# Attention and a mixture of experts on one core: three chunks of the last sequence sorted by expert, and VectorE adding the last weights

## The chip, the core and the metric

The kernel runs on one NeuronCore of a Trainium2 chip. A core has a matrix engine (TensorE, PE in the profile; its weight loads are PEld) and three engines for elementwise work: VectorE (DVE), ScalarE (ACT) and GpSimd (POOL). SyncE (SP) computes nothing here: it issues DMAs, and GpSimd issues the indirect ones. Each engine executes its own instructions in order and waits on semaphores for the others. SBUF is the on-chip memory with 128 partitions; PSUM, which the matmuls write, has eight banks of 128 x 512 fp32.

The metric is the time of one execution on the device in microseconds (us), taken as the median over runs.

## What is computed

All data is fp32: B = 4 sequences of S = 1024 tokens with D = 512 features, 16 heads of 32, and E = 8 experts of rank R = 64.

```python
x = _layernorm(x + _L0_attn_ref(x, wq, wk, wv, wo))   # softmax(q k^T) v, without a scale, then wo
logits = x_flat @ Wr.T + br                           # (4096, 8)
probs = softmax(logits)
expert_idx, expert_weight = argmax(probs), max(probs)
h = einsum('nd,erd->ner', x_flat, A)                  # A: (8, 64, 512)
y = einsum('ner,eor->neo', h, B) / 64                 # B: (8, 512, 64)
x = _layernorm(x + y[n, expert_idx[n]] * expert_weight)
```

A token needs one expert only. The reference computes all eight and picks one; a kernel may sort the tokens by expert, so that a tile of 128 tokens needs the weights of one expert, or multiply by all eight (E x R = 512 columns, as wide as D) and mask what isn't wanted.

## The kernel before

**Names.** A *unit* u is one sequence b and one group g of four heads, u = 4b + g, 16 in all; LAST = 12 is the first unit of the last sequence. A *query chunk* c or n is QC = 256 tokens; a sequence has four (NQ), and eight key tiles of 128 (NK). N = 272.

**The main loop** (L1000 to L1018) goes over steps i. A step does, in this order on every engine's queue: `early[i]` (loads on SP), `ahead[i]`, `weigh(i - 16)`, `scores(i)`, then, on every fourth step (a *busy* step), `settle` of four steps ago and `combine`, then `small[i]`, and last `fill[i]`. `keep_order` fixes the order in which the program issues the instructions as the order of each engine, so a waiting instruction holds up all that stands behind it on its engine.

- `scores(s)` computes 128 x 512 scores for each of the four heads of a unit (L290) and their row maxima on VectorE (L292). Only the maxima are kept. There are 256 such steps, 0 to 255; after step 255 there are none.
- `weigh(s)` computes the scores again, the other way round and with the maxima already subtracted: four matmuls put the negated maxima into four banks (L321), sixteen add key tile by queries (L330), and four exps on ScalarE (L340) write two key tiles of weights, `probs` (4 buffers). GpSimd adds the weights up into `dens`: one add of 128 x 1024 for the first pair of key tiles (L343), two for each later pair (L351). `weigh(s)` stands at step s + 16, so it runs in steps 16 to 271.
- `added(u, c)` says how many of the eight key tiles GpSimd adds: all, but six in the last chunk of the last sequence. `settle` sums `dens`, and with it the tiles that were not added, over the partitions by matmuls with ones (L385), and VectorE takes the reciprocal (L388) and scales the attention output `both` to `aT` (L390).
- `combine` multiplies weights and values on PE (L366) and copies the result to `both` (L374).
- `fill[i]` holds *pieces*: projections and the expert work. A planner (L916 to L955) puts each piece at a step between its `first` and its `last`, so that the steps get a similar number of PE cycles; `SHORTEST` is the least level that it fills a step to. A piece's `then` list puts further calls into the `small` (or `ahead`) list of a step so many steps later.

In sequences 0 to 2 the chunks of one unit follow each other; in the last sequence all four units do chunk 0, then all do chunk 1, and so on (L206, L208). Chunk n of the last sequence is therefore complete about every 16 steps: chunk 0 near step 224, chunk 3 at step 272.

**Sequences 0 to 2** (class `After`). `load` takes the tokens x from DRAM into tiles of tag "h" (8 buffers of 128 x 514: 512 features, the gate, and the token's place in the output). `project` adds the attention output times wo; `norm`, `choose` and `gate` layernorm two tiles, choose the expert and write the gate. When all eight tiles are done, `count` works out for every token its row in the order of experts: matmuls with a triangle of ones (L507 to L516), then some fifteen small VectorE operations, which give the row numbers `slot` and for every sorted tile its expert, `whose` (L551). `scatter` writes a tile by an indirect DMA on GpSimd's queue to the DRAM tensor `sorted_x[b]`, of NX = 16 tiles of 128 rows: a tile holds tokens of one expert, and rows that no token takes hold a place that lies out of bounds, because 1 MB writes from `nothing` were issued before (L839 to L842).

The sorted tiles are then done in pairs. For pair k: `load_tokens` reads two tiles back into buffers of tag "h" (SP, and it waits for all scatters), `load_up` and `load_down` read the expert's number into an SP register (`value_load`) and load that expert's weights, `turn_tokens` transposes on PE (L601) with copies on ScalarE, `up` (L608) and `down` (L617) multiply, and VectorE adds (L620). A step piece (`step(x)`) does `up` of pair x - 1, `down` of pair x - 2 and `turn_tokens` of pair x. The pair that had its `down` gets `weigh_y` (statistics on VectorE, `rs` on GpSimd) in the `ahead` list one step later, `norm_y` (ScalarE) two steps later and `store`, two indirect DMAs on GpSimd's queue, three steps later.

**The last sequence** (class `Last`). Each of the four chunks is done with all experts. Two chunks at a time lie in the place of `wv` (`places["h"]`), which is no longer needed. After `project`, `norm` and the choice, `turn` transposes the chunk, four `up` pieces multiply with all of `wu` (512 columns, L715), `turn_one` and `mask` spread the choice over the columns (L723) and multiply, four `down` pieces multiply with `wd` (L730), and `finish` layernorms and writes the tokens to `out` in order, by plain DMAs on SP.

Of the kernel before, what the change touches and what calls it, by code (L numbers as in the profile page):

```python
# [41 lines left out]
def attention_then_experts(  # L42
# [62 lines left out]
    wq_sb, load_wq = weight("wq", wq)  # L105
# [60 lines left out]
    sorted_x = [dram.tile([NX * P, W], F32, tag=f"sorted{b}", name=f"sorted{b}") for b in range(B - 1)]  # L166
# [146 lines left out]
    def weigh(s):  # L313
# [25 lines left out]
        for j, ps in enumerate(tiles):  # L339
            act.activation(pr[:, :, j, :], ps.rearrange("p (k q) -> p k q", q=QC), AF.Exp)  # L340
        if kp == 0:
            dens[u, c] = work.tile([P, GH * QC], F32, tag="dens", name="dens")
            pool.tensor_add(  # L343
# [4 lines left out]
        else:  # L348
            for k in range(2):
                if 2 * kp + k < added(u, c):  # L350
                    pool.tensor_add(dens[u, c], dens[u, c], pr[:, k].rearrange("p j q -> p (j q)"))  # L351

    def added(u, c):

        return NK if u < LAST or c < NQ - 1 else NK - 2
# [104 lines left out]
    class After:  # L460


        def __init__(self, b):
            self.b = b
            self.h, self.mv, self.rs, self.raw, self.ex = {}, {}, {}, {}, {}
# [4 lines left out]
        def load(self, n):  # L470
            for t in (TQ * n, TQ * n + 1):
                h = self.h[t] = work.tile([P, W], F32, tag="h", name="h", bufs=NT)
# [21 lines left out]
        def choose(self, n):  # L494
            if n == 0:
                self.one = work.tile([P, NT + 1, E], BF16, tag="one", name="one", bufs=1)
                pool.memset(self.one[:, NT], 0.0)
            self.ex[n] = choose(self.raw[n], self.one[:, ts(n, TQ), :])
# [4 lines left out]
        def count(self):  # L503

            whole = bank()
            ps = whole[:, : (NT + 1) * E].rearrange("p (t e) -> p t e", e=E)
            pe.matmul(ps, before, self.one, start=True, stop=False)  # L507
            for t in range(NT):
# [3 lines left out]
                    self.one[:, t, :].unsqueeze(1).to_broadcast((P, NT - t, E)),  # L512
                    start=False,
                    stop=(t == NT - 1),
                )

            at = [(NT + 1) * E]

            def room(n):
                at[0] += n  # L520
                return whole[:, at[0] - n : at[0]]

            tiles, place, slot, whose = room(E), room(2 * E), room(NT), room(NX)
            every = (P, NT, E)
# [3 lines left out]
                ps[:, NT, :].unsqueeze(2).to_broadcast((P, E, NT)),  # L528
# [6 lines left out]
            base = work.tile([P, E], F32, tag="base", name="base")  # L535
            dve.tensor_copy(base, place[:, :E])
            dve.tensor_add(ps[:, :NT], ps[:, :NT], base.unsqueeze(1).to_broadcast(every))
            dve.tensor_mul(wide[:, :NT], ps[:, :NT], self.one[:, :NT])
            dve.tensor_reduce(slot, wide[:, :NT], axis=AX.X, op=ALU.add)
            self.slot = work.tile([P, NT], U32, tag="slot_i", name="slot_i")  # L540
            dve.tensor_copy(self.slot, slot)

            dve.tensor_tensor(
                wide[:, :, : E - 1],
                place[:, E : 2 * E - 1].unsqueeze(1).to_broadcast((P, NX, E - 1)),
# [22 lines left out]
        def load_tokens(self, k):  # L568
            assert len(self.scatters) == NT
# [75 lines left out]
        def step(self, x):  # L645

            if 0 <= x - 1 < NT:
                self.up(x - 1)
            if 0 <= x - 2 < NT:
                self.down(x - 2)  # L650
            if x < NT:
                self.turn_tokens(x)

    places = {}

    class Last:


        def __init__(self, n):
            self.n = n  # L660
            self.h = [places["h"][:, (TQ * n + i) % C, :] for i in range(TQ)]
# [124 lines left out]
    for i, (u, c, kp) in enumerate(weights):  # L786
# [3 lines left out]
        elif kp == KP - 1:  # L790
            later(i + NS + 1, 3 * 4 * QC, settle, i)
# [23 lines left out]
    for n in range(1, NQ):  # L815
        for pair in ((0, 1), (2, 3)):
# [5 lines left out]
            for g in pair:  # L822
                Piece(lambda g=g, x_in=x_in: project_q(LAST + g, x_in), HALF, first, last, load=x_in)
# [11 lines left out]
    rest = [After(b) for b in range(B - 1)]  # L835
    for b, r in enumerate(rest):
        end = start_of(C * b + C)
        for i in range(4):
            part = sorted_x[b].rearrange("(i j p) w -> i p j w", p=P, i=4)[i]  # L839
            early[start_of(b * C + i) + 6].append(  # L840
# [3 lines left out]
        for t in range(NT):  # L844
            n, i = divmod(t, TQ)
            for half in range(2):
                then = []
                if i == TQ - 1 and half == 1:
                    then = [(2, 0, r.norm, n), (3, 0, r.choose, n), (4, 0, r.gate, n)]
# [206 lines left out]
```

## Time and profile before

| what | value |
|---|---|
| time, median of 3 runs | 1501.81 us (1500.35 to 1504.54) |
| the profiled execution | 1507.33 us |
| its span, first to last instruction | 1505.6 us |
| granted TensorE clock, mean over the span | 0.993 of full speed |
| GpSimd's adds of weights, L351 | 376 of 2358 ns: 886.6 us |
| GpSimd's adds of weights, L343 | 64 of 2355 ns: 150.7 us |
| VectorE's maxima, L292 | 1024 of 683 ns: 636.1 us |
| ScalarE's exps, L340 | 1024 of 603 ns: 528.1 us |

The page of a profile gives each engine's busy time and its share of the span, then the groups of instructions by line. A record reads, for instance, "L601 MATMUL bank<-ident,x": line 601, output `bank`, inputs `ident` and `x`; then partitions x elements of each, the type, and how many records (x8). In a timeline a row begins with its start and its length in us, and may end with the idle time before it and what ended that. A table by stretch gives the busy time of every engine between two points of the span.

### The profile page before, as it was taken

Reading aid. Unit: us, or ns where it says so; the run is one execution under the profiler, and the core shown is the slowest. Engines: PE = TensorE matmul, PEld = TensorE weight load, DVE = VectorE, ACT = ScalarE, POOL = GpSimd, SP = SyncE. Lnnn points to the kernel's source line nnn. Section 1 sums busy time; section 2 is a strip of 40 time slices with the busy share of each in tenths; the row PEclk is TensorE's granted clock in tenths of the full one; section 3 lists DMA queues with packets and bytes.
Section 4 is the critical chain, followed back from the end, with each engine's and each line's share of the span. In section 5 each row is a group of like instructions: output and inputs, shape, how many; then the busy total and the mean of one; then the engine's idle time right before and its main releaser. Section 6 shows DMA issues by size and latency. Waiting matters only on the chain. (4 is left out here: it accounts for less than half of the span.)

```text
span 1505.6 us, 36958 instructions
## 1 busy us (share of the span) xinstructions
PE 1463.2 (97%) x15091; PEld 953.4 (63%) x15091; DVE 960.0 (64%) x1797; ACT 741.7 (49%) x1519; POOL 1210.5 (80%) x935
## 2 busy tenths in 40 slices
PE   8999999999999999999999999999999999999986
PEld 6666666666665666666666666666666566666655
DVE  2546666666666567676676557677678667786523
ACT  1125555554444565555444455555554555556631
POOL 2019999998877889899887798999998899899850
PEclk9999999999999999999999999999999999999998
DMA  7422212122101522442111252441310221122100
GB/s 238 140 84 72 70 45 72 44 85 85 57 16 57 191 84 82 132 134 75 40 43 39 89 176 68 133 126 50 126 58 30 92 93 51 42 86 73 37 2 28
DMA packets 93050, 122.09 MB, mean 81 GB/s; under 512 B 7607, under 2 KB 68039, under 8 KB 92880
## 3 DMA queue, kind: packets, MB, share of 16 engines
q1 hardware_dynamic: 84672, 103.93, 21.6%
q0 software_dynamic: 6096, 13.69, 2.5%
q8 instruction: 119, 1.95, 0.5%
q10 hardware_dynamic: 2112, 2.10, 0.4%
q14 instruction: 51, 0.42, 0.1%
HBM read 92.34 MB, written 33.63 MB: 84 GB/s over the span
## 5 line engine op out<-in xcount | busy, mean ns | idle before, releaser
L351 POOL TENSOR_TENSOR dens<-dens,probs 128x1024 f32<-128x1024 f32 x376 | 886.6, 2358 | 100.9 <-ACT probs L340 79.4
L292 DVE TENSOR_REDUCE top<-bank 128x1 f32<-128x512 f32 x1024 | 636.1, 683 | 425.3 <-PE bank L290 424.8
L340 ACT ACTIVATE probs<-bank 128x512 f32<-128x512 f32 x1024 | 528.1, 603 | 272.7 <-PE bank L330 261.0
L290 PE MATMUL bank<-k,q 32*128 32x512 f32 x2048 | 286.9, 594 | 3.3 <-DVE whose_i L551 3.3
L330 PE MATMUL bank<-q,k 32*128 32x256 f32 x4096 | 266.6, 374 | 0.0
L366 PE MATMUL bank<-probs,v 128*32 128x256 f32 x4096 | 236.6, 383 | 0.0
L330 PEld LDWEIGHTS bank<-q,k 32*128 32x128 f32 x4096 | 201.5, 184 | 17.4 <-issue 1.9
L366 PEld LDWEIGHTS bank<-probs,v 128*32 128x32 f32 x4096 | 130.9, 111 | 95.1 <-ACT probs L340 14.6
L343 POOL TENSOR_TENSOR dens<-probs 128x1024 f32<-128x1024 f32 x64 | 150.7, 2355 | 18.0 <-ACT probs L340 17.8
L257 PE MATMUL bank<-xT,wq 128*128 128x256 f32 x512 | 128.5, 395 | 7.6 <-DMA xT<-in_xt 7.0
L388 DVE RECIPROCAL bank<-bank 128x256 f32<-128x256 f32 x64 | 112.6, 1759 | 33.2 <-PE bank L385 33.0
L290 PEld LDWEIGHTS bank<-k,q 32*128 32x128 f32 x2048 | 111.6, 184 | 27.8 <-DVE whose_i L551 5.8
L257 PEld LDWEIGHTS bank<-xT,wq 128*128 128x128 f32 x512 | 93.7, 192 | 54.8 <-ACT probs L340 33.1
L446 PE MATMUL bank<-wo,aT 128*128 128x264 f32 (+1 forms) x512 | 122.1, 390 | 5.6 <-ACT probs L340 4.6
L267 PE MATMUL bank<-xT,wk 128*128 128x256 f32 x512 | 123.5, 386 | 3.2 <-ACT probs L340 3.1
L276 PE MATMUL bank<-wv,xT 128*128 128x256 f32 (+1 forms) x512 | 124.5, 391 | 1.2 <-ACT probs L340 0.4
L446 PEld LDWEIGHTS bank<-wo,aT 128*128 128x128 f32 x512 | 94.6, 190 | 41.6 <-ACT probs L340 26.0
L267 PEld LDWEIGHTS bank<-xT,wk 128*128 128x128 f32 x512 | 95.2, 191 | 36.8 <-ACT probs L340 25.0
L374 ACT COPY both<-bank 128x256 f32<-128x256 f32 x64 | 23.8, 372 | 191.4 <-PE bank L366 175.7
L276 PEld LDWEIGHTS bank<-wv,xT 128*128 128x128 f32 x512 | 93.8, 190 | 36.1 <-ACT probs L340 19.2
L321 PE MATMUL bank<-mT,ones_b 3*128 3x512 bf16 x1024 | 106.0, 385 | 1.3 <-ACT probs L340 0.3
L321 PEld LDWEIGHTS <-ones_b 3*128 3x128 bf16 x1024 | 26.9, 91 | 91.0 <-issue 90.8
(123 smaller groups left out, 969.2 us busy)
## 6 DMA issues: line engine op xcount, KB each, us to landing
xT<-in_xt SPq DMA_DIRECT2D x98, 512.0 KB, 3.5
sorted<-nothing SPq DMA_DIRECT2D x12, 1028.0 KB, 6.6
x<-sorted SPq DMA_DIRECT2D x48, 257.0 KB, 3.6
h<-in_x SPq DMA_DIRECT2D x32, 256.0 KB, 3.7
wa<-in_wa SPq DMA_DIRECT2D x48, 128.0 KB, 2.2
wb<-in_wb SPq DMA_DIRECT2D x48, 128.0 KB, 3.4
out<-h SPq DMA_DIRECT2D x8, 256.0 KB, 2.0
wo<-in_wo POOLq DMA_DIRECT2D x1, 1024.0 KB, 6.3
```

The source lines that it names most:

```text
L257: pe.matmul(ps, wq_sb[:, c, ts(units[u][1], P)], x.x[:, c, :], start=(c == 0), stop=(c == C - 1))
L267: pe.matmul(ps, wk_sb[:, c, ts(units[u][1], P)], x.x[:, c, :], start=(c == 0), stop=(c == C - 1))
L276: pe.matmul(ps, x.x[:, c, ts(t, P)], wv_sb[:, c, columns(h)], start=(c == 0), stop=(c == C - 1))
L290: pe.matmul(ps, q[r, ts(t % TQ, P)], kT[u][r, ts(n, 512)], start=True, stop=True)
L292: dve.tensor_reduce(top[i][:, here // 2, j, n : n + 1], ps, axis=AX.X, op=ALU.max, negate=True)
L321: pe.matmul(ps.rearrange("p (k q) -> p k q", q=QC), ones_b[r, :], m[r, :].unsqueeze(1).to_broadcast((NP, 2, QC)), start=True, stop=False,)
L330: pe.matmul(ps[:, ts(k, QC)], kT[u][r, ts(2 * kp + k, P)], qT[u, c][r, :], start=False, stop=(k == 1),)
L340: act.activation(pr[:, :, j, :], ps.rearrange("p (k q) -> p k q", q=QC), AF.Exp)
L343: pool.tensor_add(dens[u, c], pr[:, 0].rearrange("p j q -> p (j q)"), pr[:, 1].rearrange("p j q -> p (j q)"),)
L351: pool.tensor_add(dens[u, c], dens[u, c], pr[:, k].rearrange("p j q -> p (j q)"))
L366: pe.matmul(ps[j * HD : (j + 1) * HD, :], v[:, k, col : col + HD], probs[u, c, k // 2][:, k % 2, j, :], start=(k == 0), stop=(k == NK - 1),)
L446: pe.matmul(ps, aT[b, c, n][:, ts(i, P)], wo_sb[:, c, columns(half)], start=(c == 0), stop=(c == C - 1))
```

## The change

It has four parts.

1. **Three chunks sorted.** The last sequence gets an `After` too, with nt = 6 token tiles (chunks 0 to 2) and nx = 14 sorted tiles, so 7 pairs. Its token tiles don't take buffers of tag "h": `place(t)` puts the first four where `wv` was and two where `wq` was (`places["late"]`, taken once the last query projection is done). Sorted tiles, when they are read back, do use tag "h". `Last` does chunk 3 alone.
2. **Steps by hand.** Projections of the last sequence, its pairs (`TAIL`) and chunk 3's work get narrow or single steps. `norm_y` and `store` follow one and two steps behind a pair (`GAP`), not two and three. A fourth `sorted_x` is written with `nothing`.
3. **VectorE adds the last weights.** From step 256 on, where there are no more maxima, the adds L343 and L351 go to VectorE. `added` leaves one key tile out of the sum in chunk 2 of the last sequence (two in unit 15), so `settle` takes these by matmuls; chunk 3 leaves out two, as before. Where eight are added, `settle` stays four steps behind `combine`; with seven it goes two steps behind it, with six one.
4. **Counting in two parts**, for all sequences: the part that gives the experts of the tiles is now `assign`, on a bank of its own and one step later. `choose`, `gate`, `count` and `assign` avoid busy steps (`step_without`). Lines after L341 stand one to thirty lines further down: the adds of weights are L344 and L352 in the changed kernel, the transposes of `turn_tokens` L607.

```diff
-    wq_sb, load_wq = weight("wq", wq)
+    wq_sb, load_wq = weight("wq", wq, W - D)
...
-    sorted_x = [dram.tile([NX * P, W], F32, tag=f"sorted{b}", name=f"sorted{b}") for b in range(B - 1)]
+    sorted_x = [dram.tile([NX * P, W], F32, tag=f"sorted{b}", name=f"sorted{b}") for b in range(B)]
...
+        adder = pool if s + NS < len(maxima) else dve
...
-            pool.tensor_add(
+            adder.tensor_add(
...
-                    pool.tensor_add(dens[u, c], dens[u, c], pr[:, k].rearrange("p j q -> p (j q)"))
+                    adder.tensor_add(dens[u, c], dens[u, c], pr[:, k].rearrange("p j q -> p (j q)"))
 
     def added(u, c):
 
-        return NK if u < LAST or c < NQ - 1 else NK - 2
+        if u < LAST or c < NQ - 2:
+            return NK
+        return NK - 1 if c < NQ - 1 and u < U - 1 else NK - 2
...
+            self.nt, self.nx = (NT, NX) if b < B - 1 else (NT - TQ, NX - TQ)
...
-                h = self.h[t] = work.tile([P, W], F32, tag="h", name="h", bufs=NT)
+                h = self.h[t] = work.tile([P, W], F32, tag="h", name="h", bufs=NT) if self.b < B - 1 else place(t)
                 sync.dma_start(h[:, :D], x[self.b, ts(t, P), :])
...
+            nt = self.nt
...
-            at = [(NT + 1) * E]
-
-            def room(n):
-                at[0] += n
-                return whole[:, at[0] - n : at[0]]
-
-            tiles, place, slot, whose = room(E), room(2 * E), room(NT), room(NX)
-            every = (P, NT, E)
+            tiles, place, slot = (whole[:, 128 + 32 * i : 160 + 32 * i] for i in range(3))
+            tiles, place, slot = tiles[:, :E], place[:, : 2 * E], slot[:, :nt]
+            every = (P, nt, E)
...
+            self.base = work.tile([P, 2 * E], F32, tag="base", name="base")
+            dve.tensor_copy(self.base, place)
...
             self.slot = work.tile([P, NT], U32, tag="slot_i", name="slot_i")
-            dve.tensor_copy(self.slot, slot)
-
+            dve.tensor_copy(self.slot[:, :nt], slot)
+
+        def assign(self):
+
+            ps = bank()
+            ends, whose = ps[:, : E - 1], ps[:, 32 : 32 + NX]
+            dve.tensor_copy(ends, self.base[:, E : 2 * E - 1])
+            wide = work.tile([P, NX, E], F32, tag="wide", name="wide", bufs=1)
             dve.tensor_tensor(
                 wide[:, :, : E - 1],
-                place[:, E : 2 * E - 1].unsqueeze(1).to_broadcast((P, NX, E - 1)),
+                ends.unsqueeze(1).to_broadcast((P, NX, E - 1)),
...
     places = {}
+
+    def place(t):
+
+        return places["h"][:, t, :W] if t < C else places["late"][:, t - C, :W]
 
...
-            self.h = [places["h"][:, (TQ * n + i) % C, :] for i in range(TQ)]
+            self.h = [place(TQ * n + i)[:, :D] for i in range(TQ)]
...
-            later(i + NS + 1, 3 * 4 * QC, settle, i)
+            later(i + NS + 3 - (NK - added(u, c)), (NK - added(u, c) + 1) * 4 * QC, settle, i)
...
-    rest = [After(b) for b in range(B - 1)]
+    rest = [After(b) for b in range(B)]
+
+    def step_without(k):
+
+        return lambda i: i + k + (i + k in busy)
+
+
+    TAIL = [(N - 7, N - 6), (N - 6, N - 4), (N - 4, N - 3), (N - 3, N - 2)]
+    TAIL += [(N + i, N + i) for i in (0, 2, 3, 4, 6)]
+    GAP = [2] * (B - 1) + [1]
     for b, r in enumerate(rest):
         end = start_of(C * b + C)
         for i in range(4):
             part = sorted_x[b].rearrange("(i j p) w -> i p j w", p=P, i=4)[i]
-            early[start_of(b * C + i) + 6].append(
+            early[min(start_of(b * C + i), start_of(LAST)) + 6 + (b == B - 1) * i].append(
                 lambda part=part: sync.dma_start(part, nothing.unsqueeze(1).to_broadcast((P, NX // 4, W)))
...
-        for t in range(NT):
+        for t in range(r.nt):
             n, i = divmod(t, TQ)
+            first = end - NS + KP * (n + 2)
+            last_ = first + 5
+            if b == B - 1:
+                first = start_of(LAST) + NS * (n + 1) + KP
+                last_ = first + 5
+                if n == NQ - 2:
+                    first = last_ = start_of(LAST) + NS * (n + 1) + 1 + i
             for half in range(2):
                 then = []
                 if i == TQ - 1 and half == 1:
-                    then = [(2, 0, r.norm, n), (3, 0, r.choose, n), (4, 0, r.gate, n)]
-                    if n == NQ - 1:
-                        then += [(4, 600, r.count)]
+                    if b < B - 1 or n < NQ - 2:
+                        then = [(2, 0, r.norm, n), (step_without(2), 0, r.choose, n), (step_without(4), 0, r.gate, n)]
+                    else:
+                        then = [(1, 0, r.norm, n), (1, 0, r.choose, n), (2, 0, r.gate, n)]
+                    if b < B - 1 and n == NQ - 1:
+                        then += [(step_without(3), 600, r.count), (step_without(4), 0, r.assign)]
                         then += [(5 + k // 2, 0, r.scatter, k) for k in range(NT)]
+                    elif b == B - 1 and n == NQ - 2:
+                        then += [(2, 600, r.count), (3, 0, r.assign)]
+                        then += [(3 + k // 3, 0, r.scatter, k) for k in range(r.nt)]
                 p = Piece(
                     lambda r=r, t=t, half=half: r.project(t, half),
                     HALF,
-                    end - NS + KP * (n + 2),
-                    end - NS + KP * (n + 2) + 5,
+                    first,
+                    last_,
                     after=[(p, 0)] if p else (),
                     load=loads.setdefault((b, n), lambda r=r, n=n: r.load(n)),
                     then=then,
                 )
-        for k in range(NT + 2):
+        for k in range(r.nx // 2 + 2):
+            if b < B - 1:
+                first, last_ = end + 17 + 3 * k, end + 25 + 4 * k
+            else:
+                first, last_ = TAIL[k]
             p = Piece(
                 lambda r=r, k=k: r.step(k),
                 3 * 2200,
-                end + 17 + 3 * k,
-                end + (25 if b < B - 2 else 23) + 4 * k,
-                after=[(p, 3 if k else 11)],
-                then=[(-1, 0, r.weigh_y, k - 2), (2, 0, r.norm_y, k - 2), (3, 0, r.store, k - 2)] if k >= 2 else [],
+                first,
+                last_,
+                after=[(p, 3 if b < B - 1 else 1) if k else (p, 11 if b < B - 1 else 6)],
+                then=[(-1, 0, r.weigh_y, k - 2), (GAP[b], 0, r.norm_y, k - 2), (GAP[b] + 1, 0, r.store, k - 2)]
+                if k >= 2
+                else [],
             )
             r.steps.append(p)
...
-    for n in range(NQ):
-        a = start_of(LAST) + NS * n + NS - 1
-        p, ups, downs = None, [], []
...
+    n, p, ups = NQ - 1, None, []
+    for i in range(TQ):
+        for half in range(2):
+            then = []
+            if i == TQ - 1 and half == 1:
+                then = [(1, 0, on_last(n, "norm")), (1, 0, on_last(n, "choose")), (2, 0, on_last(n, "weigh"))]
+                then += [(2, 300, on_last(n, "turn_one")), (3, 2200, on_last(n, "turn"))]
+            p = Piece(
+                on_last(n, "project", i, half),
+                HALF,
+                N + 1,
+                N + 1,
+                after=[(p, 0)] if p else (),
+                load=loads.setdefault((B - 1, n), on_last(n, "load")),
+                then=then,
+            )
+    for k in range(C):
+        ups.append(Piece(on_last(n, "up", k), HALF, N + 5, N + 5, after=[(p, 4)]))
+    q = Piece(on_last(n, "mask"), 1024, N + 6, N + 6, after=[(o, 1) for o in ups])
+    for i in range(TQ):
+        for half in range(2):
+            done = i == TQ - 1 and half == 1
+            then = [(1, 0, on_last(n, "finish"))] if done else []
+            Piece(on_last(n, "down", i, half), HALF, N + 7, N + 7, after=[(q, 1)], then=then)
...
-    def take(name, pool_, tag, bufs, src=None):
-        t = places[name] = pool_.tile([P, C, D], F32, tag=tag, name=name, bufs=bufs)
+    def take(name, pool_, tag, bufs, cols, src=None):
...
-    last_k, last_v = (1 + max(p.step for p in pieces if p.kind == kind) for kind in "kv")
-    early[last_k].append(lambda: take("wu", const, "wk", 1, wu))
-    early[last_v].insert(0, lambda: take("h", const, "wv", 1))
-    early[start_of(LAST) + 10].append(lambda: take("wd", work, "v", 3, wb.rearrange("e r d -> (e r) d")))
+    last_q, last_k, last_v = (1 + max(p.step for p in pieces if p.kind == kind) for kind in "qkv")
+    early[last_k].append(lambda: take("wu", const, "wk", 1, D, wu))
+    early[last_v].insert(0, lambda: take("h", const, "wv", 1, D + E))
+    early[last_q].insert(0, lambda: take("late", const, "wq", 1, W))
```

## The prediction, made before the changed kernel had run

> **What bounds the kernel now.** First the page's busy times, then busy time by stretch, then the engines' timelines in the stretch that the change rewrites. A "step" is one pass of the main loop; I place steps in time by the group of four L321 matmuls that opens each `weigh`.
>
> ```profile
> PE 1463.2 (97%) x15091; PEld 953.4 (63%) x15091; DVE 960.0 (64%) x1797; ACT 741.7 (49%) x1519; POOL 1210.5 (80%) x935
> ```
> ```profile
> 1206.80:1378.00 171.20, 169.15 (x1876) 108.46 (x1876) 127.62 (x243) 95.61 (x193) 158.57 (x116) 1.00 0.21 66
> 1378.00:1451.00 73.00, 69.39 (x758) 46.56 (x754) 29.63 (x67) 45.40 (x90) 60.59 (x49) 0.98 0.11 38
> 1451.00:1505.60 54.60, 39.32 (x255) 30.13 (x254) 17.82 (x47) 10.25 (x20) 9.64 (x15) 0.90 0.06 20
> ```
> The columns are length, then busy PE, PEld, DVE, ACT, POOL, clock, DMA share, GB/s. The rows are steps 224 to 255, steps 256 to 270, and step 271 to the end. PE is full in the first, GpSimd close behind (93%); in the last a third is waiting. So PE work removed early pays until GpSimd is the bound; later the waits decide.
>
> **PE work removed and added.** All durations are pitches on PE's timeline. A dense chunk costs 4 `up` pieces of 1.83 (two L715 in 3.65 us), 4 `down` of 1.83, `turn` 1.3, `mask` 0.5, `turn_one` 0.3: 16.7 us. Three go: 50.1 us. A sorted pair costs this, one line each for up, down and turn:
>
> ```profile
> 1383.99 1.09 PE L608 MATMUL bank<-xsT,wa 128*64 128x128 f32 x16
> 1385.02 1.13 PE L617 MATMUL bank<-wb,u 64*128 64x512 f32 x4
> 1386.08 1.09 PE L601 MATMUL bank<-ident,x 128*128 128x128 f32 x8
> ```
> That is 3.15 us, seven times: 22.0 us. `count` adds 0.8; three settles get one more tile at 0.5 (24 L385 records take 1.43 us at 1399.06): 1.5. Net **25.8 us less PE work**.
>
> **Steps 224 to 255.** Removed here: all of chunk 0, and `turn`, `turn_one` and half of `up` of chunk 1: 16.7 + 1.6 + 3.7 = 22.0; added 1.5; about 3 us of PE waiting for the norms before those `turn`s goes too. But the built order leaves steps 236, 238, 241 and 242 without any filler, so GpSimd is late next. In steps 236 to 247 it has 19 adds at 2.41 us (7 + 6 + 6; pitch of pairs, 4.80), three stores of a pair at 2.65, four `rs` at 1.2 and two splits at 1.4: 61 us against 51 of PE. Four `probs` buffers and settles one or two steps later absorb all but 4 to 8 us; I take 6. Sum: -22.0 + 1.5 - 3 + 6 = **-17 us** (-22 to -11).
>
> **Steps 256 to 270.** PE work: 15 `weigh` at 1.19, three `combine` at 3.6, four settles 5.7, projections 7.6, `turn_m` and `count` 1.0, pair work 15.6: 58.6 us against 73.0 long before. Against it stand new waits, read from the built order of each engine and priced with these rows:
>
> ```profile
> 1427.36 1.41 DVE L620 SCALAR_TENSOR_TENSOR x<-bank,x 128x512 f32<-128x512 f32 x2 [0.62 <-PE bank L617]
> ...
> 1430.70 0.15 DVE L408 TENSOR_SCALAR y_mv<-y_mv 128x1 f32<-128x1 f32 x1
> ```
> ```profile
> 1294.94 1.09 POOL L635 DMA_INDIRECT out<-x  x1 [0.57 <-issue]
> ```
> ```profile
> 1297.98 1.42 SPq L572 DMA_DIRECT2D x<-sorted  x2
> ```
> `down`'s VectorE part with the following statistics takes 3.5 us. A buffer of tag "h" that `store` begins to empty at 1294.94 is reloaded from 1297.98; the second load of the two issues near 1299.1 and lands 3.6 us later by the page: 7.7 us from store to tokens.
>
> VectorE's add of 128x1024 is not in the trace. [...] I take 1.2 us, with 1.07 and 2.2 as ends.
>
> - Step 257: VectorE's queue is add (exps of 256 end), reciprocal, multiply: 1.2 + 1.77 + 0.45. PE's projection waits **1.6 us** for aT.
> - `count` comes after add, reciprocal and gate; slots are ready 30 us into the stretch. Scatters 1 to 3 issue, but on POOL the `rs` of b=2's pair 5 stands before 4 to 6 and waits for VectorE (two adds, `assign` 0.9, 3.5 of pair 5) until 37; ACT's norm, and behind it the exps of step 264, wait as well. The settle of 264 needs dens behind the same work: **3.5 us**. Scatters end near 42, and the first tokens land at 48, where PE stood from 43: **4.8 us**. Smaller ones: 1.2.
> - Step 270 is the place that decides. Tokens of pair 3 need a buffer of b=2's pair 7, whose `store` is queued on POOL at step 271, behind the `rs` of b=3's pair 1, which needs `down`(1), which PE does just before `turn_tokens`(3). So PE waits through VectorE's statistics, 1.2 of `rs`, and 7.7: at least 3.5 + 1.2 + 7.7 = 12.4 us with VectorE free. It is not: from the exps of 268 it has five adds (6.0), a reciprocal with its multiply (2.3) and three times 3.5 in one row, 18.8 us. PE arrives at 69.8, tokens at 89.6: **19.8 us**.
>
> 58.6 + 1.6 + 3.5 + 4.8 + 1.2 + 19.8 = 89.5. After a gap the clock is low, as here (same columns as above):
>
> ```profile
> 1466.50:1470.10 3.60, 0.50 (x4) 0.18 (x2) 3.00 (x9) 0.81 (x2) 1.52 (x5) 1.00 0.00 0
> 1470.10:1477.00 6.90, 6.80 (x27) 5.32 (x28) 1.36 (x6) 2.01 (x5) 0.00 (x0) 0.75 0.00 0
> ```
> A quarter of 6.9 is 1.7 us for each long gap: two here, 3.4. Sum 93 against 73: **+20 us** (+10 to +28).
>
> **From step 271.** PE: `weigh`, `combine`, settle 6.2; pairs 12.5; projection 7.6; last chunk's `turn`, `up`, `mask`, `down` 16.5: 42.8. Tokens of pair 6 wait for a store queued behind the last chunk's `rs` (+5.3, and 1.7 of clock); mask 1.5; the last norm and output as now (last PE record ends 1495.8, span 1505.6) 9.8. Sum 61.1 against 54.6: **+6.5 us** (+2 to +10). The stores of the last pair end inside the 9.8.
>
> **Before step 224.** `assign` gets a bank of its own and `count` sits earlier: the three PE waits for whose_i (3.3 us before L290) should go, **-3.5** (-5 to 0). Four more `nothing` writes of 1 MB each sit on SP between xT loads that are issued three steps (15 us) ahead: 0; one landing, 6.6 us, if that cover fails. The place-of copies (0.2 us each) lie under GpSimd's slack, and the larger `late` tile and x loads are issued a chunk early: 0.
>
> **Sum.** -17 + 20 + 6.5 - 3.5 = +6, with the ends' uncertainty lying more to the long side of the VectorE row: I take +8. The profiled execution took 1507.3 us (span 1505.6), 5.5 above the median of the runs, 1501.8. So 1515 for a profiled execution, and **1510 us** for the median.
>
> **Rivals.**
> - *PE's sum carries.* 97% busy PE speaks for it; the queue order against. Without the 270 backlog beyond 12.4 (-7.4), without the waits of 264 and 265 and their clock (-10), and with GpSimd's lag absorbed (-6): 1510 - 23 = 1487. The full PE sum would be 1476. This is also the case if the pair-3 load did not wait for the late store.
> [...]
> - *GpSimd keeps steps 224 to 255 as they are.* If its lag reaches the exps through the four buffers, -17 shrinks to -9: 1518. For it: 93% busy already.
>
> **Chances.** Forecast (own range 1502 to 1518) 0.47; PE's sum 0.25; VectorE 0.18; GpSimd 0.10. Within 0.3% of 1501.8, about what a measurement of this kernel can tell, ends at 1506.3: a quarter of the forecast's mass and a fifth of the first rival's fall there. So faster 0.20, same 0.18, slower 0.62. The range for 8 in 10 is 1488 to 1525.
>
> **What would show it.** Steps 224 to 255 take about 154 us with GpSimd over 95% busy; L352 (the adds) on VectorE has mean 1.2 us; PE idles near 20 us in one piece before an L607 transpose, with the x load of pair 3 waiting for out<-x on SP; gaps of 3 to 5 us stand before the first L607 of b=3 and before pair 6; the last stretch is near 61 us. I am wrong if the one long gap is under 12 us or absent, or if VectorE's adds are far from 1.2 us.

## The result, and the profile after

The changed kernel takes **1523.53 us** (median of 4 runs, 1522.21 to 1525.23) against 1502.38 us before (4 runs): **1.0141** times as long, 95% interval 1.0123 to 1.0160. It is slower, by 21 us where 8 had been forecast.

The page's busy times, and then busy time by stretch, in the columns and at the steps of the prediction (224 to 255, 256 to 270, 271 to the end):

```profile
PE 1451.4 (95%) x15100; PEld 933.0 (61%) x15100; DVE 992.9 (65%) x1853; ACT 749.7 (49%) x1527; POOL 1186.0 (78%) x949
```
```profile
1197.43:1360.55 163.12, 156.70 (x1792) 93.53 (x1788) 123.01 (x232) 90.01 (x179) 150.54 (x114) 1.00 0.21 66
1360.55:1453.19 92.64, 68.48 (x775) 41.52 (x771) 55.96 (x102) 46.94 (x92) 33.82 (x45) 0.86 0.27 82
1453.19:1520.90 67.71, 48.67 (x327) 34.02 (x326) 28.65 (x75) 21.46 (x40) 20.37 (x35) 0.80 0.27 85
```

| stretch | before | after | difference | forecast |
|---|---|---|---|---|
| up to step 224 | 1206.8 | 1197.4 | -9.4 | -3.5 |
| steps 224 to 255 | 171.2 | 163.1 | -8.0 | -17 |
| steps 256 to 270 | 73.1 | 92.6 | +19.6 | +20 |
| step 271 to the end | 54.6 | 67.7 | +13.1 | +6.5 |

The spans differ by 15.3 us. The medians differ by 21.2, because the profiled execution of before was a long one of its kind (1507.3) and that of the changed kernel was not (1522.7). The excess of the former lies ahead of step 224: e3 below has 1199.5 us there, and its later stretches agree with before within 0.2 us.

What decided step 270 is seen in one piece of the changed kernel's timeline (start, length, engine, operation, idle time before and its releaser):

```profile
1436.60 2.08 PE L623 MATMUL bank<-wb,u 64*128 64x512 f32 x4
...
1437.15 1.31 POOL L402 TENSOR_SCALAR var<-y_mv 128x2 f32<-128x2 f32 x1 [2.45 <-DVE y_mv L410]
1437.16 2.47 DVE L352 TENSOR_TENSOR dens<-dens,probs 128x1024 f32<-128x1024 f32 x2
1438.54 1.67 POOL L403 TENSOR_TENSOR rs<-var,power 128x2 f32<-128x2 f32 x1
1439.56 1.40 DVE L626 SCALAR_TENSOR_TENSOR x<-bank,x 128x512 f32<-128x512 f32 x2
...
1442.94 0.22 POOL L402 TENSOR_SCALAR var<-y_mv 128x2 f32<-128x2 f32 x1 [2.46 <-DVE y_mv L410]
1443.24 0.71 POOL L403 TENSOR_TENSOR rs<-var,power 128x2 f32<-128x2 f32 x1
1444.03 0.20 POOL L404 TENSOR_TENSOR rs<-y_mv,rs 128x2 f32<-128x2 f32 x1
1444.85 1.04 POOL L641 DMA_INDIRECT out<-x  x1 [0.63 <-issue]
1446.20 0.99 POOL L641 DMA_INDIRECT out<-x  x1 [0.30 <-issue]
1447.03 1.66 SPq L578 DMA_DIRECT2D x<-sorted  x2
...
1449.68 1.11 PE L607 MATMUL bank<-ident,x 128*128 128x128 f32 x4 [11.00 <-DMA x<-sorted]
...
1452.18 1.09 PE L607 MATMUL bank<-ident,x 128*128 128x128 f32 x4 [1.39 <-DMA x<-sorted]
```

Read it downwards: `down` of pair 1 ends (L623); VectorE does two adds of weights that were queued first, then the pair's add and statistics; GpSimd's `rs` waits for these; behind it stand the two stores of sequence 2's last pair; when the first store has landed, 2.1 us after its issue began, SP's load of pair 3 leaves; PE, idle for 11.0 us, gets the first tile, and after 1.39 us more the second.

### The profile page after: what moved, and what is told of

The parts are those of the page before. It is cut to its first block, busy times and chain, and to the rows that moved or that the text cites. A ratio compares the mean times of both kernels' runs of the same rounds, so it can differ in the third digit from the quotient of the medians.

```text
span 1520.9 us, 37286 instructions
## 1 busy us (share of the span) xinstructions
PE 1451.4 (95%) x15100; PEld 933.0 (61%) x15100; DVE 992.9 (65%) x1853; ACT 749.7 (49%) x1527; POOL 1186.0 (78%) x949
## 4 chain that ended last, share of the span: by engine, by line
PE 79%; POOL 7%; ACT 4%; DVE 4%; issue 3%; DMA 2%; POOLq 0%; SPq 0%; ACTq 0%; DVEq 0%
PE bank L369 13%; PE bank L290 12%; PE bank L330 12%; PE bank L276 8%; PE bank L257 8%; PE bank L267 7%; PE bank L449 7%; POOL dens L352 5%; PE bank L321 5%; ACT probs L340 3%; PE bank L388 2%; PE bank L623 2%; PE bank L607 1%; PE bank L614 1%; DVE top L292 1%
## 5 line engine op out<-in xcount | busy, mean ns | idle before, releaser
L352 POOL TENSOR_TENSOR dens<-dens,probs 128x1024 f32<-128x1024 f32 x355 | 837.7, 2360 | 92.7 <-ACT probs L340 71.8
L290 PE MATMUL bank<-k,q 32*128 32x512 f32 x2048 | 287.1, 594 | 1.2 <-DVE slot_i L541 0.8
L330 PE MATMUL bank<-q,k 32*128 32x256 f32 x4096 | 268.6, 376 | 0.0
L330 PEld LDWEIGHTS bank<-q,k 32*128 32x128 f32 x4096 | 202.7, 185 | 18.3 <-issue 2.6
L344 POOL TENSOR_TENSOR dens<-probs 128x1024 f32<-128x1024 f32 x60 | 141.4, 2356 | 8.8 <-ACT probs L340 8.5
L290 PEld LDWEIGHTS bank<-k,q 32*128 32x128 f32 x2048 | 110.9, 184 | 26.5 <-issue 5.4
L276 PEld LDWEIGHTS bank<-wv,xT 128*128 128x128 f32 x512 | 93.9, 190 | 34.6 <-ACT probs L340 17.5
L321 PE MATMUL bank<-mT,ones_b 3*128 3x512 bf16 x1024 | 108.5, 387 | 3.6 <-ACT probs L340 1.7
L641 POOL DMA_INDIRECT out<-x x62 | 63.3, 1021 | 33.0 <-issue 15.3
## 6 DMA issues: line engine op xcount, KB each, us to landing
wv<-in_wv ACTq DMA_DIRECT2D x2, 512.0 KB, 13.1
```

The costliest lines, as they stand in the source:

```text
L276: pe.matmul(ps, x.x[:, c, ts(t, P)], wv_sb[:, c, columns(h)], start=(c == 0), stop=(c == C - 1))
L290: pe.matmul(ps, q[r, ts(t % TQ, P)], kT[u][r, ts(n, 512)], start=True, stop=True)
L321: pe.matmul(ps.rearrange("p (k q) -> p k q", q=QC), ones_b[r, :], m[r, :].unsqueeze(1).to_broadcast((NP, 2, QC)), start=True, stop=False,)
L330: pe.matmul(ps[:, ts(k, QC)], kT[u][r, ts(2 * kp + k, P)], qT[u, c][r, :], start=False, stop=(k == 1),)
L344: adder.tensor_add(dens[u, c], pr[:, 0].rearrange("p j q -> p (j q)"), pr[:, 1].rearrange("p j q -> p (j q)"),)
L352: adder.tensor_add(dens[u, c], dens[u, c], pr[:, k].rearrange("p j q -> p (j q)"))
```

## The experiments

Ratios are to the kernel before on the same chip in the same series. "L330 to L330" is the time from the first L330 record of one step to that of the next, which is taken as a step's length; the stretches are cut at the first L321. A *theory* and its *rival* are the two outcomes that each run was to tell apart.

**e1: places of their own for the first three pairs.**

```diff
-                self.x[k, i] = work.tile([P, W], F32, tag="h", name="x", bufs=NT)
+                if self.b == B - 1 and k < 3:
+                    self.x[k, i] = place(2 * k + i)
+                else:
+                    self.x[k, i] = work.tile([P, W], F32, tag="h", name="x", bufs=NT)
```

> The changed kernel, but sorted pairs 0 to 2 of the last sequence are read back into the six places that held its unsorted tokens (free once all six scatters are done), so pair 3 takes a buffer that was emptied long before. Theory (the late store): the 12.4 us that PE waits for the tokens of pair 3 go, with about 1.7 us of lower clock behind them; stretch 256 to 270 takes about 79 us instead of 92.6 and the time falls by 13 to 15 us, to about 1509.5. Rival 1 (VectorE's row of adds and statistics decides there): a wait for VectorE takes its place, and the time falls by less than 6 us. Rival 2 (the next token load is as late): the gap moves to pair 4 or 5 and the time stays within 3 us.

1517.26 us, ratio 1.0078 (1.0060 to 1.0096). In its timeline of PE, the transposes of pair 3 (L610 here) follow `down` at once:

```profile
1441.59 2.08 PE L626 MATMUL bank<-wb,u 64*128 64x512 f32 x4
1443.60 1.57 PE L610 MATMUL bank<-ident,x 128*128 128x128 f32 x8
1445.10 0.39 PE L321 MATMUL bank<-mT,ones_b 3*128 3x512 bf16 x3
1447.95 0.53 PE L321 MATMUL bank<-mT,ones_b 3*128 3x512 bf16 x1 [2.46 <-ACT u L621]
```

Steps 256 to 270 take 80.3 us instead of 92.6: the theory held for the wait. The last line shows a smaller one in its place (ScalarE's copy of `u` stands behind a norm that waits for `rs`), and the last stretch, in which that wait lies, grew by 3.0. So the gain is less than the 13 to 15 us of the theory: of the ratio's 1.4% the late store is 0.6%, some 9 us.

**e2: the last 20 adds back on GpSimd** (`adder = pool`).

> The changed kernel with the last 20 adds of weights back on GpSimd (2.41 us each there, 1.23 us on VectorE). Theory (queues, the store of the late pair behind everything on GpSimd): GpSimd gets 48 us more in 90, the rs and the stores of the pairs stand behind adds, the wait for the tokens of pair 3 grows from 12.4 to 15 to 25 us, and the time rises by 3 to 15 us. Rival (VectorE's adds are what costs): the waits of PE for VectorE in steps 256 to 270 (1.6, 2.1, 1.6, 1.4 and 0.9 us) go and the time falls by 3 to 8 us.

1528.07 us, ratio 1.0143 (1.0121 to 1.0166): as the changed kernel, so neither the loss nor the gain shows in the time. The theory's wait came about, at the low end of its 15 to 25 us:

```profile
1455.40 1.12 PE L607 MATMUL bank<-ident,x 128*128 128x128 f32 x4 [15.58 <-DMA x<-sorted]
1457.96 1.08 PE L607 MATMUL bank<-ident,x 128*128 128x128 f32 x4 [1.44 <-DMA x<-sorted]
```

That is 17.0 us instead of 12.4. PE's other waits in steps 256 to 270 came to 9.2 us instead of 11.7 (one of them, 3.4, is now for GpSimd's `dens`), and the stretch takes 93.9 us instead of 92.6: what grew and what fell nearly cancel.

**e3: part 4 alone on the kernel before** (`count` and `assign` with their steps as in the diff).

> The kernel before with part 4 alone: count in two parts, the second on its own bank one step later, both beside busy steps. Theory (this part gave the 9.4 us before step 224): the time falls by 8 to 10 us against the kernel before. Rival (only PE's 3.3 us of waits for whose_i go, and the rest is the kernel before's profiled execution being a long one): it falls by 3 to 4 us.

1501.19 us against 1505.30: ratio 0.9969 (0.9958 to 0.9979). The rival's size was right. The ten runs lie within 1500.26 and 1502.46, the fifteen of the kernel before on this chip between 1501.85 and 1509.61. **This version beats both kernels**, the one before by 0.3%. With it as the base, the other three stretches of the table are 171.2, 73.3 and 54.6 us, as before.

**e4: part 3 alone on the kernel before** (adder, `added`, steps of `settle`).

> The kernel before with part 3 alone: the last adds on VectorE, one or two key tiles of chunk 2 left to settle. Theory (the part is worth something by itself, since GpSimd ends its row of adds in steps 260 to 268 last): steps 256 to 270 take 66 to 70 us instead of 73, and the time falls by 3 to 7 us. Rival (settle and the pairs' statistics stand behind the adds on VectorE): it rises by 2 to 5 us. Steps before 240 are those of the kernel before, so its time there shows how much of 1206.8 us to step 224 is usual.

1515.01 us, ratio 1.0067 (1.0045 to 1.0088): the theory fell, the loss of 10 us is about twice the most that the rival allowed. Steps 224 to 255 take 175.4 us (e3: 171.2), 256 to 270 take 75.9 (73.3). In the first of these stretches PE has 24 `settle` matmuls more (1.3 us busy), and L290 is busy for 38.9 us instead of 36.3; what holds L290 was not tested. GpSimd's relief gives nothing back.

**e5 to e8: GpSimd relieved, and the end.** All but e8 have e1's places. e5, e7 and e8 have fewer adds:

```diff
-        if u < LAST or c < NQ - 2:
+        if u < LAST or c == 0:
             return NK
-        return NK - 1 if c < NQ - 1 and u < U - 1 else NK - 2
+        return NK - 1 if c == 1 else NK - 2
```

e6 and e7 have the last pair's store in the step of its norm:

```diff
-(GAP[b] + 1, 0, r.store, k - 2)
+(GAP[b] + (b < B - 1 or k - 2 < 6), 0, r.store, k - 2)
```

e7 adds 1 to both gaps where `b == B - 1 and k - 2 < 3`.

> The kernel with the six spare places, and GpSimd relieved: in chunk 1 of the last sequence one key tile, in chunk 2 two of every unit are left to settle instead of GpSimd (7 adds, 16.9 us of GpSimd, against 3.5 us more of PE; settles of chunk 1 stand two steps behind combine). The planner then also puts the last two pairs of sequence 2 five and three steps earlier. Theory (GpSimd is full in steps 236 to 255 and sets their length): stretch 224 to 256 falls from 164.6 to 155 to 159 us, although it holds one pair more (3.2 us), and the whole by 6 to 10 us, to 1507 to 1511. Rival (PE, or the banks that VectorE and ScalarE hold, set it): the stretch rises by 3 to 7 us with PE's work.

> The kernel with the six spare places, and the store of the very last pair put right behind its norm, so that on GpSimd it stands ahead of the last chunk's rs. Theory (GpSimd's end waits about 8 us after its last indirect DMA, as the trace of the changed kernel shows 7.9 us between that issue's end and its next event): the span ends 4 to 5 us earlier after the last matmul (9.8 us instead of 14.5 us). Rival (only the landing of the last store counts): 1 us or less.

> Spare places, GpSimd relieved, the last store early, and for the last sequence's first three pairs norm and store one step later, so that ScalarE does not stand in front of the exps waiting for rs. Theory: the sum of the two kernels above and 3 to 5 us from PE's 2.5 us waits for exps and for the copy of u in steps 270 and 271: 1498 to 1504. Rival (the waits only move): 1505 to 1509, no faster than the two together.

> The changed kernel with only the adds of GpSimd relieved, no spare places. Theory: stretch 224 to 256 as in the kernel with both; and since the planner then stores the last pair of sequence 2 at step 267 instead of 271, the 12.4 us wait for its buffer goes too, so that this kernel and the one with both agree within 3 us. Rival (the buffers of pairs 4 to 6 are as late): it stays 8 us or more above it.

| | us | ratio | 95% interval | steps 224 to 255 | step 270, L330 to L330 | last PE record to end of span |
|---|---|---|---|---|---|---|
| changed | 1523.53 | 1.0141 | 1.0123 to 1.0160 | 163.1 | 22.5 | 14.5 |
| e5 | 1514.89 | 1.0091 | 1.0077 to 1.0106 | 170.4 | 9.5 | 14.5 |
| e6 | 1507.74 | 1.0041 | 1.0025 to 1.0057 | 163.1 | 11.2 | 11.5 |
| e7 | 1507.79 | 1.0043 | 1.0030 to 1.0056 | 168.8 | 5.3 | 11.5 |
| e8 | 1517.85 | 1.0108 | 1.0093 to 1.0122 | 170.2 | 9.5 | 14.4 |

e5: the GpSimd theory fell. GpSimd is busy for 48.2 of 63.3 us in steps 236 to 247 (changed: 57.7 of 60.5), and the stretch grew by 7, as the rival said; about 5 us of that is PE's work (`settle`, and parts of pairs moved in), the rest waiting.

e8 confirms e1 by another route: with fewer adds the planner puts the late store at step 267 instead of 271, and the wait for tokens at step 270 is gone; it agrees with e5 within 3 us. But in e5, e6 and e8 another wait, of 4.0 to 4.1 us, stands in the same step before the fourth L321, as here in e5:

```profile
1448.42 0.37 PE L321 MATMUL bank<-mT,ones_b 3*128 3x512 bf16 x1 [4.05 <-ACT u L621]
```

e6: the end is 3.0 us shorter, not 4.7; where the other 1.6 us lie is said in the last section. e7 misses its 1498 to 1504 and is no faster than e6. Its later norms did what they were to do: the wait for `u` is gone, and step 270 takes 5.3 us instead of e5's 9.5. But it also carries e5's edit, with which steps 224 to 255 take 5.7 us more than in e6.

**e9 to e12, all on e6.** e9 leaves GpSimd's adds out:

```diff
-                if 2 * kp + k < added(u, c):
+                if 2 * kp + k < added(u, c) and not 236 <= s + NS < 256:
```

e10 moves two `turn_tokens` from `step` to the `small` list one step later. e11 is e2's edit where step 270 no longer waits (`adder = pool`). e12, in `weigh_y`, with `still` a constant tile:

```diff
-            for i in range(2):
-                stats(mv, i, self.x[k, i][:, :D])
+            if self.b == 2 and k < 5:
+                mv = still
+            else:
+                for i in range(2):
+                    stats(mv, i, self.x[k, i][:, :D])
```

> The kernel with spare places and the early last store, but in steps 236 to 255 every add of weights except the first of a chunk is left out (about 26 adds, 63 us of GpSimd; the sums of weights are then too small); the order of all other work is the same. GpSimd theory (it is full there and sets the length): steps 236 to 255 fall from 102.4 to about 92 us, PE's own work. Theory of the empty steps (a step without filler is set by the banks that the next weigh needs and ScalarE's exps must read first): they stay within 2 us of 102.4.

> The kernel with spare places and the early last store; the 1.09 us of transposes of two pairs of sequence 2 move from the full steps 237 and 240 to the empty steps behind them, 238 and 241. Nothing else changes: PE, GpSimd and VectorE have the same work. Theory of the empty steps: an empty step has more than 1.1 us of waiting, which the transposes fill, so steps 236 to 247 fall by 1.5 to 2.5 us from 60.4. GpSimd or VectorE theory: they stay within 0.5 us. The whole kernel by the same amount, which its time may not show.

> The kernel with spare places and the early last store, and the last 20 adds on GpSimd again. VectorE theory (in steps 256 to 270, where 58.6 us of PE's work take 77.2, the waits are for VectorE, which has 24.5 us of adds in its row): the stretch falls to 70 to 74 us. Rival (with the adds on GpSimd the rs, scatters and stores queue behind them, for the same waits or more): it takes 77 to 84 us.

> The kernel with spare places and the early last store; for the first five pairs of sequence 2, whose statistics stand in steps 238 to 255, VectorE's statistics (2.1 us a pair, 10.3 us in all) are left out and constants taken instead, so the second layernorm of these rows is wrong; all else is the same. VectorE theory (it is busy 85 to 92% of steps 236 to 243, and maxima, which free the banks of the scores, stand behind statistics and reciprocals in its row): steps 236 to 255 fall from 102.4 us by 4 to 9 us. Theory of ScalarE and the banks (exps behind norms): they fall by less than 1.5 us.

Steps 236 to 247, first in the changed kernel, then in e9 (columns as above, GpSimd's busy time is the last with a count):

```profile
1258.10:1318.60 60.50, 57.91 (x670) 33.00 (x668) 49.52 (x97) 35.65 (x70) 57.69 (x43) 1.00 0.21 66
```
```profile
1260.90:1321.30 60.40, 57.83 (x668) 32.98 (x664) 49.45 (x97) 35.64 (x70) 22.12 (x30) 1.00 0.21 66
```

GpSimd goes from 57.7 to 22.1 us, and nothing else moves; steps 236 to 255 take 102.2 us (e6: 102.4). It was busy for 95% of steps 236 to 247 and not their bound. e12 takes 10 us from VectorE; steps 236 to 255 go from 102.4 to 101.6, so VectorE's statistics are not the bound either. In e10 the two transposes shortened the full steps by 1.03 us each and lengthened the empty ones by 1.22 and 1.31: that theory, as I had put it, fell. But ScalarE copies what is transposed (1.07 us), and that copy stands between two rounds of exps, so the edit had added to the very thing that was suspected. e11: ratio 1.0047 (1.0031 to 1.0063), steps 256 to 270 take 75.2 us instead of 77.2 in e6, or of 78.9 in e9 and e10, which ran in e11's series and have e6's work in these steps: between the two forecasts. VectorE's adds cost 2 to 4 us there; they saved nothing.

**e13: matmuls without a use, and without a copy by ScalarE, in four empty steps** (on e6).

```diff
+        more = {236: 2, 238: 2, 241: 4, 242: 4}.get(i, 0)
+        if more:
+            ps = bank()[:, :QC]
+            for c in range(more):
+                pe.matmul(ps, ident, wo_sb[:, c, :QC], start=(c == 0), stop=(c == more - 1))
+            dve.tensor_copy(seen, ps[:, :8])
```

> The kernel with spare places and the early last store, with matmuls added whose result nobody needs (128x256, 0.48 us each by the rows of L257): two each in the empty steps 236 and 238 (1.0 us), four each in 241 and 242 (1.9 us), 5.8 us of PE in all. From the first L330 of a step to that of the next, these steps take 3.70, 3.32, 3.23 and 3.37 us now, for 2.05 us of PE's own work. Theory of the floor (an empty step waits for ScalarE's exps to free the banks, 3.3 us whatever PE does): 236 and 238 stay within 0.3 us of these times, and 241 and 242 take 3.97 us, like every step with one half of a projection; 1.0 to 2.0 us in all. Rival (PE's work adds up): each step grows by all of its matmuls, 5 to 6 us in all.

| L330 to L330 of step | 236 | 238 | 241 | 242 |
|---|---|---|---|---|
| changed | 3.70 | 3.32 | 3.23 | 3.37 |
| e9, adds left out | 3.70 | 3.32 | 3.23 | 3.35 |
| e12, statistics left out | 3.70 | 3.32 | 3.23 | 3.37 |
| e10, transposes in 238 and 241 | 3.70 | 4.54 | 4.54 | 3.37 |
| e13, 1.0, 1.0, 1.9, 1.9 us of matmuls | 3.70 | 3.32 | 3.97 | 4.24 |

The theory held to the hundredth in three of four; 242 also holds the 0.33 us of `turn_m`. Step 238 on PE's timeline, in the changed kernel (with ScalarE's four exps) and in e13:

```profile
1268.36 1.03 PE L330 MATMUL bank<-q,k 32*128 32x256 f32 x16
1269.22 1.02 PE L290 MATMUL bank<-k,q 32*128 32x512 f32 x8
1269.55 2.07 ACT L340 ACTIVATE probs<-bank 128x512 f32<-128x512 f32 x4 [0.68 <-PE bank L330]
1270.20 1.84 PE L321 MATMUL bank<-mT,ones_b 3*128 3x512 bf16 x4
1271.67 1.23 PE L330 MATMUL bank<-q,k 32*128 32x256 f32 x16
```
```profile
1270.52 1.03 PE L330 MATMUL bank<-q,k 32*128 32x256 f32 x16
1271.38 1.03 PE L290 MATMUL bank<-k,q 32*128 32x512 f32 x8
1272.36 1.13 PE L1047 MATMUL bank<-wo,ident 128*128 128x256 f32 x4
1273.43 0.79 PE L321 MATMUL bank<-mT,ones_b 3*128 3x512 bf16 x4
1273.84 1.25 PE L330 MATMUL bank<-q,k 32*128 32x256 f32 x16
```

Four L321 take 0.4 us when nothing holds them (0.39 at 1268.13 in the changed kernel); here they take 1.84, and the added matmul fits inside, with the next L330 again 3.32 us after the last. `weigh` and `scores` take four banks each, eight in all. Without a filler that takes a bank, the next L321 want the banks of the last `weigh`, and each is free when its exp has read it: the L321 behind step 236, at 1261.08, wait 0.83 us for `probs`. So the round L330, four exps (2.06 us), L321 sets a floor of 3.2 to 3.7 us under these steps, though PE's own work in them and step 252 together is 10.6 us, some 2.1 for each. That PE has time to spare in them is shown by e13, and that neither GpSimd's adds nor VectorE's statistics set the floor by e9 and e12. That the exps do is read from the timeline and the order of the banks, and fits e10; no run made the exps shorter.

## Why the prediction was right and wrong

**Right: direction, and the mechanism of step 270.** The load of pair 3, the late store in front of it, the `rs` in front of that: each is in the timeline, and e1 and e8 take the wait away by two routes. Its size was the floor named for a free VectorE, 12.4 us (11.0 + 1.39), not 19.8. That it agrees to the tenth is luck: two adds still stood in front of pair 1 on VectorE (until 1439.6, 0.9 us after `down` had ended), and PE did half of the transposes before the second tile came. The longer backlog on VectorE was not there: PE had been held up before, by seven waits of 0.9 to 2.5 us, so VectorE had caught up, and stood idle for 7.9 us before its add at 1424.69.

**The split of this stretch was wrong, and its sum right by luck.** The stretch came out at 92.6 against 93. The long wait is 7.4 us shorter. The other waits came to 11.7 us against 11.1, but not where they had been forecast: before the first transposes of the last sequence, at 1408.61, PE waits 1.40 us, not 4.8. PE is busy for 68.5 us, where work and clock had been put at 62.0. The clock is part of that:

```profile
1431.00:1455.00 24.00, 9.11 (x68) 5.61 (x64) 11.48 (x23) 7.05 (x13) 11.45 (x13) 0.56 0.28 77
```

Around the long wait the granted clock is 0.56; laid over PE's busy time, the trace's clock costs an estimated 6.3 us in this stretch, against 3.4. The other 3.6 us of the excess were not taken apart.

**Right: part 4.** Forecast -3.5, measured -4.1 (e3).

**Wrong: "GpSimd is late next", at 6 us, in steps 224 to 255.** This is the step that failed, in cause and in size. Counted step by step, about 19 us of PE work went (21 of dense work, less 1.7 more of `settle`), and about 11 us came back as waiting, where the sum had a net 3 (-3 + 6). Busy 95% of the time, GpSimd looked like the bound of steps 236 to 247, and the rival built on it even came near the total (-9; measured -8.0), for a reason that e9 refutes there.

The schedule had been noted to leave steps 236, 238, 241 and 242 without filler; what was not asked is how long such a step must be. With 252 they take 17.3 us for 10.6 of PE's work, so 6.7 us are waiting; before, one step was of this kind, with 0.9. The difference is half of the 11. Another 2.2 us is a single wait for GpSimd after all, but in step 226, ahead of the steps of e9:

```profile
1209.90 0.40 PE L303 MATMUL bank<-ident_b,sm 128*128 128x128 bf16 x4 [2.40 <-POOL sm L197]
```

Two adds of weights stand in front of the split of the maxima (`sm`) on GpSimd, and PE comes there earlier than before, since step 225 now holds one half of a projection and not two. The last 3 us lie mainly in steps 237, 246, 250 and 254, and were not taken apart. The floor could be read in the trace of before, whose step 234 has no filler either:

```profile
1256.66 1.03 PE L330 MATMUL bank<-q,k 32*128 32x256 f32 x16
1257.52 1.03 PE L290 MATMUL bank<-k,q 32*128 32x512 f32 x8
1258.48 0.40 PE L303 MATMUL bank<-ident_b,sm 128*128 128x128 bf16 x4
1258.94 1.37 PE L321 MATMUL bank<-mT,ones_b 3*128 3x512 bf16 x4
1259.92 0.48 PE L330 MATMUL bank<-q,k 32*128 32x256 f32 x2
```

It takes 3.27 us from L330 to L330, and steps with one half of a projection take 3.98: the last half, 1.93 us, is worth 0.7 when it goes.

**Wrong: "the stores of the last pair end inside the 9.8".** The end took 14.5 us: 4.7 of the 6.6 by which the last stretch was mis-sized. The last store was queued behind the last chunk's `rs`, which is 3.0 of it (e6), and GpSimd then took 1.6 us longer to finish than before (last section). PE's part of the stretch was 53.2 us against a sum of 51.3. The wait of 5.3 us for the tokens of pair 6 did not come (PE waits 0.94 us before that transpose, at 1481.33); the clock, 0.80 over the stretch, costs an estimated 6.9 us of PE's busy time against 1.7.

**Wrong: the way to the median.** The 5.5 us between the profiled execution of before and the median were taken off the changed kernel's time as well. Its profiled execution was no such outlier.

**VectorE's add.** 1.22 us (20 of them, 1.21 to 1.25) against 1.2 forecast. In the trace of before there is no such add; two shorter operations there, 0.68 us for 128x512 (L725) and 0.42 for 128x256 (L390), differ by 1.0 ns an element, which gives an estimate of 1.2 us for 1024. No run shows an add at the prediction's ends of 1.07 and 2.2 us, and its 0.18 for VectorE was the author's chance of much longer adds, which did not come. The longer operations are on GpSimd: beside an add its two small ones take 1.31 and 1.67 us, alone 0.22 and 0.71, both pairs in the timeline above, and the adds keep their length. It is so in all three such places of this trace; what holds GpSimd there, no run shows.

**Together:** 9.0 (steps 224 to 255) and 6.6 (the end), less 0.4 (steps 256 to 270) and the 2 that the sum had been rounded up by, is the 13 us between forecast and result. The 5.9 us by which the time before step 224 fell further than forecast and the 5.5 us of the way to the median nearly cancel.

## What to carry to other kernels

Before a piece of work is counted as saved, find in the trace a step that lacks it already: in this loop, which hands PSUM banks from engine to engine, the steps without filler (234 before, 236, 238, 241 and 242 after) took 3.2 to 3.7 us, and the last half of a projection in a step was worth 0.7 of its 1.93 us. GpSimd, busy for 95% of steps 236 to 247, was not their bound; so leave the work out for one run and see whether anything moves, and look in the list of waits for the places where it does hold something up. When a buffer is reloaded, follow the store that empties it back through every queue that it stands in, to what those queues wait for.

## What was not expected of the hardware

These are the last entries of the changed kernel's timeline; its span ends at 1520.9:

```profile
1509.89 1.05 POOL L641 DMA_INDIRECT out<-x  x1 [0.63 <-issue]
1510.13 1.06 SPq L755 DMA_DIRECT2D out<-late  x2
1511.24 0.99 POOL L641 DMA_INDIRECT out<-x  x1 [0.30 <-issue]
```

The last store lands about 1.1 us after its issue ends, but GpSimd's next event comes 7.8 us after it. The trace lists what GpSimd executes there, at the end of the program: three DRAIN instructions, of which the first is long (shortest, median and longest in ns). In the changed kernel, in the kernel before and in e6:

```profile
L1085 POOLq DRAIN  x3: 51/103/9788, 1510.3 to 1520.6; - x3
```
```profile
L1052 POOLq DRAIN  x3: 51/103/6452, 1498.4 to 1505.4; - x3
```
```profile
L1092 POOLq DRAIN  x3: 51/103/8085, 1495.0 to 1503.7; - x3
```

The expectation of e6 laid this time to an indirect DMA being the last thing on GpSimd. The traces do not bear that out: the long DRAIN ends 7.84 to 7.86 us after GpSimd's last work in all twelve kernels that sort the last sequence, whether that work is a store (changed, e1, e2, e5, e8) or the last chunk's `rs` (e6, e7, e9 to e13), and 6.22 us after it in the three that do not (before, e3, e4). So e6 gained its 3.0 us because GpSimd's last work ended 2.9 us after PE's last record instead of 5.8, and the 1.6 us left over against before are the longer DRAIN. The twelve issue 92 indirect DMAs and the three 72; whether that sets the length, and what the DRAIN waits for, no run here shows.
